# A four-layer graph network on one core: layer 0 of the first batches by the adjacency itself, zero products while it loads, another order of loads

## The chip, the core and the metric

The kernel runs on one core of a Trainium2 chip. The core has a matrix engine (TensorE, PE in the profile, with its weight loads as PEld), a vector engine (DVE), a scalar engine (ACT), GpSimd (POOL), a sync engine (SP) that here only issues transfers, and 16 DMA engines behind the queues of SP and ACT. All data is float32, but for the masks (bfloat16). The metric is the device time of one run in microseconds, lower is better. Three runs of the kernel before took 1646.48, 1648.0 and 1648.28 us.

## The reference

`x` is 32 batches of 512 nodes with 128 features, `adj` one 512 x 512 matrix, mostly zeros, positive where there is an edge, the diagonal included. Four layers follow one another, each as `x = x + layer(relu(layernorm(x)))`. Layer 0 is the one that the change touches:

```python
A_hat = adj + eye(n)
d = sum(A_hat, axis=-1) ** (-0.5)
A_norm = d[:, None] * A_hat * d[None, :]
out = einsum('nm,bmc->bnc', A_norm, x)
out = einsum('bnc,oc->bno', out, W) + b
```

Layer 1 is a gated graph unit of five steps; each step multiplies `adj` with the state `h` of a batch and puts the result and `h` through gates: `z = sigmoid(..)`, `r = sigmoid(..)`, `hv = tanh(.. + (r*h) @ u5.T)`, `h = (1-z)*h + z*hv`. Layers 2 and 3 are graph attention: `e = leaky_relu(e_src + e_dst)`, masked by `adj`, softmax over the neighbours, and the weighted sum of `h = x @ W`; layer 2 has an elu behind it.

## The kernel before

**Tiles.** The 512 nodes of a batch lie as four chunks of 128 partitions, so a batch is a tile of 128 x (4 x 128). `adj` is loaded as four chunks of 128 rows (L250, on the queues of SP and ACT in turn), and PE turns each chunk, block by block, into `adjT` (L285; ACT copies the result out of PSUM, L287). Beside it DVE sums the rows to `deg` (L288, L290), and GpSimd raises it to the power -0.5: `dinv` (L291).

**The normalized matrix.** Before layer 0 can start, `anT`, the turned A_norm, is built: PE turns `dinv` into a row spread over all partitions (L300), and for each of four chunks DVE multiplies `adjT` by `dinv` of the partition and by that row (L308) and adds dinv squared on the diagonal block (L311).

**Layer 0** (`gcn`) works on pairs of batches. Normalization takes the statistics on DVE (L406, L410, L411), the reciprocal root on GpSimd (L413), an offset on DVE (L420) and the scaled relu on ACT (L423). The first two pairs (batches 0 to 3) use `product`: four matmuls of 128x128 by 128x512 each (L551), one PSUM copy on ACT (L553), four small matmuls by the turned W (L572) and one addition into x on DVE (L574). All later pairs use `products`, which makes both batches of a pair at once by seven products of half size in place of eight (L516); it needs sums and differences of the halves of its two inputs, the tile `S` (L504, four DVE operations), and sums of quarters of the matrix, `made` (L325). Layer 1 (`ggnn`, `step`) uses `products` with `adjT` in each of its five steps, then the gate matmuls (L603, L604, L610, L617 and, for the candidate, L618), tanh on ACT (L606, L612, L620) and the update on DVE (L608, L622, L623, L625). At the end of layer 1 the result is added to x (L633 for the last batches).

**Attention** (`gat`) makes scores from a row of values and the masks (e, L713), multiplies (L733, for the last four batches L722), and adds the result into x (L738, L750, L752 in layer 2; L744 in layer 3). The masks are made once (L340, L342) and go through DRAM (L345, L348) to `maskT`.

**Order.** The program has no fixed loop order. `Plan` collects operations with an engine, a cost, a due time, and the values that they read and write; a value takes a buffer from a small pool when its first operation starts (two tiles `y`, eight PSUM banks, thirteen `x`). `run` walks through this list as an event queue: on each engine the ready operation with the earliest due time goes next. It tries 16 settings of two parameters, keeps the one that ends first by its own costs, and emits the instructions in that order. Each engine then executes its own list strictly in order, and an instruction that waits holds up all behind it. So a change of a cost or a due time anywhere can move operations everywhere, and the order of transfers on SP is such a list as well. Transposes of weights (`transposed`, L364, with the copies L368 and L370) and small constants have due times from -1000 to -9 and fill the start; x of batches 0 to 7 has due times from -995 on.

Of the kernel before, what the change touches and what calls it, by code (L numbers as in the profile page):

```python
# [12 lines left out]
AF = mybir.ActivationFunctionType  # L13
ALU = mybir.AluOpType

P = 128
# [5 lines left out]
NEAR = 4  # L22
EASE = 0
FAR0, FAR1 = 2, 4
LANES = 6


# [140 lines left out]
def gnn_stack(ctx: ExitStack, tc: tile.TileContext, a: dict, out: bass.AP):  # L168
# [13 lines left out]
    def flat(t):  # L182
        return t.rearrange("p c k -> p (c k)")
# [54 lines left out]

    ident = fixed([P, P], "ident")
    mhalf = fixed(SMALL, "mhalf")  # L240
    warm = fixed([P, 1], "warm")
    op("POOL", 0.8, -1000, lambda: make_identity(nc, ident.t), w=[ident])
    op("POOL", 0.1, -999, lambda: nc.gpsimd.memset(mhalf.t, -0.5), w=[mhalf])
    op("DVE", 0.1, -1000, lambda: nc.vector.memset(warm.t, 0.0), w=[warm])
    op("ACT", 1.4, -1000, lambda: nc.scalar.activation(warm.t, warm.t, AF.Tanh), w=[warm])

    adj_sb = Val("e", C)
    for c in range(C):
        e, q = (("SP", nc.sync), ("ACT", nc.scalar))[c % 2]
        op(e, 0.45, -1001, lambda c=c, q=q: q.dma_start(adj_sb.t[:, c, :], adj[c * P:(c + 1) * P, :]),  # L250
           w=[adj_sb[c]], delay=3.6)
    xs = []
    for b in range(B):
        v = Val("x", C)
        op("SP", 0.95, max(-995 + b, STEPS * b - 20) if b >= 8 else -995 + b, lambda v=v, b=b: nc.sync.dma_start(v.t, x[b].rearrange("(c p) d -> p c d", p=P)),
           w=[v], delay=3)
        xs.append(v)
    w0 = load("w0", [P, D], a["L0_gnn_W"], -993.5)
    b0 = load("b0", [P, D], bass.AP(tensor=a["L0_gnn_b"].tensor, offset=a["L0_gnn_b"].offset,
                                    ap=[[0, P], [1, D]]), -993.4)  # L260

# [6 lines left out]
    w_aug, a_pair = {}, {}  # L268
    for l, w in ((2, "L2_gnn_W"), (3, "L3_gnn_w")):
        w_aug[l] = fixed([P, D + 3], f"w_aug{l}", 2)  # L270
        op("SP", 0.45, -990.5, lambda l=l, w=w: nc.sync.dma_start(w_aug[l].t[:, :D], a[w]), w=[w_aug[l][0]], delay=2.4)
        a_pair[l] = fixed([P, 2], f"a_pair{l}", 2)
        for i, k in enumerate(("src", "dst")):
            op("SP", 0.45, -990.4, lambda l=l, i=i, k=k: nc.sync.dma_start(
                a_pair[l].t[:, i:i + 1], column(a[f"L{l}_gnn_a_{k}"])), w=[a_pair[l][i]], delay=2.4)
# [4 lines left out]
    for c in range(C):  # L280
        p = Val("bank")

        def turn_adj(c=c, p=p):
            for m in range(C):
                nc.tensor.transpose(p.t[:, m, :], adj_sb.t[:, c, m * P:(m + 1) * P], ident.t)  # L285
        op("PE", C * TURN, -800, turn_adj, r=[adj_sb[c], ident], w=[p])
        op("ACT", A, -800, lambda c=c, p=p: nc.scalar.copy(adjT.t[:, :, c * P:(c + 1) * P], p.t), r=[p], w=[adjT[c]])  # L287
        op("DVE", 0.66, -801, lambda c=c: nc.vector.reduce_sum(deg.t[:, c:c + 1], adj_sb.t[:, c, :], axis=mybir.AxisListType.X),  # L288
           r=[adj_sb[c]], w=[deg[c]])
    op("DVE", 0.1, -799, lambda: nc.vector.tensor_scalar_add(deg.t, deg.t, 1.0), w=[deg])  # L290
    op("POOL", 1.0, -1000, lambda: nc.gpsimd.tensor_tensor(dinv.t, deg.t, mhalf.t, ALU.pow), r=[deg, mhalf], w=[dinv])  # L291


    anT = fixed([P, C, N], "anT", C)
    drow = Val("bank")
    dinv2 = fixed(SMALL, "dinv2")

    def turn_dinv():
        for c in range(C):
            nc.tensor.transpose(drow.t[:, c, :], dinv.t[:, c:c + 1].to_broadcast([P, P]), ident.t)  # L300
    op("PE", C * TURN, -798, turn_dinv, r=[dinv, ident], w=[drow])
    op("DVE", 0.1, -798, lambda: nc.vector.tensor_mul(dinv2.t, dinv.t, dinv.t), r=[dinv], w=[dinv2])

    def block(t, m):
        return t[:, m, m * P:(m + 1) * P]

    for m in range(C):
        op("DVE", 0.7, -797, lambda m=m: nc.vector.scalar_tensor_tensor(  # L308
            anT.t[:, m, :], adjT.t[:, m, :], dinv.t[:, m:m + 1], flat(drow.t), op0=ALU.mult, op1=ALU.mult),
           r=[adjT, dinv, drow], w=[anT[m]])  # L310
        op("DVE", 0.26, -797, lambda m=m: nc.vector.scalar_tensor_tensor(  # L311
            block(anT.t, m), ident.t, dinv2.t[:, m:m + 1], block(anT.t, m), op0=ALU.mult, op1=ALU.add),
           r=[ident, dinv2], w=[anT[m]])

    def right_factors(mT, due):

# [9 lines left out]
                f[k][0](), quarter(*u), quarter(0, 1) if v is None else f[v][0]()),  # L326
               r=[mT, *([f[v][1]] if v else [])], w=[f[k][1]])
        return f
    of_adj, of_an = right_factors(adjT, -3), right_factors(anT, 5)


    maskT = {l: fixed([P, Q, N], f"maskT{l}", C, dtype=BF16) for l in (2, 3)}
    for l in (2, 3):
        far = Val(None, C)
        far.t = tiles(1, [Q, W, C, N], f"far_mask{l}", dram, BF16)[0]
        for c in range(C):
            part = Val("mask", 1)

            def edges(l=l, c=c, part=part):
                nc.vector.tensor_scalar(part.t, adjT.t[:, c, :], 0.0, None, op0=ALU.is_gt)  # L340
                if l == 2:
                    nc.vector.scalar_tensor_tensor(part.t[:, c * P:(c + 1) * P], block(adjT.t, c), -1.0, ident.t,  # L342
                                                   op0=ALU.mult, op1=ALU.is_lt)
            op("DVE", 0.35 if l == 3 else 0.6, 4 + l, edges, r=[adjT, ident], w=[part])
            op("SP", 0.4, 4 + l, lambda c=c, far=far, part=part: nc.sync.dma_start(  # L345
                far.t[:, :, c, :].rearrange("q i n -> (q i) n"), part.t), r=[part], w=[far[c]], delay=2.2)
        for c in range(C):
            op("SP", 0.4, 4 + l, lambda l=l, c=c, far=far: nc.sync.dma_start(  # L348
                maskT[l].t[c * W:(c + 1) * W], far.t[:, :, c, :].rearrange("q i n -> i q n")),
               r=[far], w=[maskT[l][c]], delay=2.2)  # L350

# [27 lines left out]
    w0T = transposed(-750, (one(w0), 1))  # L379
    gates = transposed(-700, (halves("w4"), 1), (one(raw["u3"]), 1), (halves("w3") + halves("w4", minus), 1), (halves("w5"), 1))  # L380
    u5T = transposed(-690, (one(raw["u5"]), 0.5))
    gats = transposed(-10, (one(w_aug[2]), 1), (one(w_aug[3]), 1))
    gate_b = {}
    for k, u, half in (("w4", "u3", True), ("w3", "u3", True), ("w5", "u5", False)):
        gate_b[k] = fixed([P, 1], "gate_b" + k)
# [5 lines left out]

    for i, l in enumerate((2, 3)):
        p = Val("bank")
        op("PE", 0.3, -9, lambda i=i, l=l, p=p: nc.tensor.matmul(p.t[:, 0, :2], gats.t[:, i, :], a_pair[l].t, start=True, stop=True),
           r=[gats, a_pair[l]], w=[p])

        def columns(l=l, p=p):
            for j, (s, f) in enumerate(((1, SLOPE), (1, 1.0 - SLOPE), (0, SLOPE - 1.0))):
                nc.vector.tensor_scalar_mul(w_aug[l].t[:, D + j:D + j + 1], p.t[:, 0, s:s + 1], f)
        op("DVE", 0.3, -9, columns, r=[p], w=[w_aug[l][1]])  # L400


    def norm_stats(b, due):
# [9 lines left out]
        op("POOL", 1.0, due, lambda: nc.gpsimd.tensor_tensor(rstd.t, ve.t, mhalf.t, ALU.pow), r=[ve, mhalf], w=[rstd])  # L413
        return mv, rstd

    def norm_relu(b, y, due):

        xb, off = xs[b], Val("off")
        mv, rstd = norm_stats(b, due)
        op("DVE", 0.1, due, lambda: nc.vector.scalar_tensor_tensor(off.t, mv.t[:, :, 0], -1.0, rstd.t, op0=ALU.mult, op1=ALU.mult),  # L420
           r=[mv, rstd], w=[off])
        for c in range(C):
            op("ACT", 0.385, due, lambda c=c: nc.scalar.activation(  # L423
                chunk(y, c), xb.t[:, c, :], AF.Relu, bias=off.t[:, c:c + 1], scale=rstd.t[:, c:c + 1]),
               r=[xb[c], off, rstd], w=[y[c * len(y.writers) // C]])
# [118 lines left out]
        copy(m1[1], r, lambda: high(m1))  # L544
        return m1, m2

    def product(h, mT, due):

        p, m = Val("bank"), Val("m")
        for c in range(C):  # L550
            op("PE", MM, due, lambda c=c: nc.tensor.matmul(flat(p.t), chunk(h, c), mT.t[:, c, :], start=(c == 0), stop=(c == C - 1)),  # L551
               r=[h[c], mT[c]], w=[p, m])
        op("ACT", A, due, lambda: nc.scalar.copy(flat(m.t), flat(p.t)), r=[p], w=[m])  # L553
        return m


    def gcn(pair, due):
        first, ys = pair[0] < 4, []
        for i, b in enumerate(pair):
            y = Val("y", C) if first else Val("pair", 2)  # L560
            norm_relu(b, y, 2 * b - 798 if pair[0] == 0 else due + i)
            op("DVE", V, due + i + 1, lambda b=b: nc.vector.tensor_add(
                xs[b].t, xs[b].t, b0.t[:, None, :].to_broadcast([P, C, D])), r=[b0], w=[xs[b]])
            ys.append(y)

        ms = [product(y, anT, due + i + 1) for i, y in enumerate(ys)] if first else products(*ys, of_an, due + 1)
        for i, (b, m) in enumerate(zip(pair, ms)):
            p = Val("bank")

            def out_mm(m=m, p=p):  # L570
                for c in range(C):
                    nc.tensor.matmul(p.t[:, c, :], m.t[:, c, :], w0T.t[:, 0, :], start=True, stop=True)  # L572
            op("PE", C * MM1, due + i + 1.5, out_mm, r=[m, w0T], w=[p])
            op("DVE", V, due + i + 1.5, lambda b=b, p=p: nc.vector.tensor_add(flat(xs[b].t), flat(xs[b].t), flat(p.t)),  # L574
               r=[p], w=[xs[b]])


    def ggnn(pair, due):
# [177 lines left out]


    for b in range(0, B, 2):
        gcn((b, b + 1), STEPS * b - 10)
        ggnn((b, b + 1), STEPS * b)  # L760
        for i in range(2):
            gat(b + i, 2, STEPS * (b + i) + LANES * (STEPS - 1) + 3)
# [33 lines left out]
```

The softmax here doesn't subtract the row's maximum and nothing guards it: scores larger than these inputs give would overflow.

## Time and profile before

| | |
|---|---|
| time of three runs | 1646.48 to 1648.28 us, median 1648.0 |
| span of the profiled run | 1645.1 us |
| PE busy | 1620.7 us, 99% |
| DVE busy | 1373.5 us, 83% |
| ACT busy | 722.0 us, 44% |
| first PE instruction | 4.64 us |
| last PE instruction ends | 1640.1 us |

A line of the time line gives start, duration (from the start of the first to the end of the last of a run of like instructions), engine, line, operation, output and input with shapes, and how many; a bracket gives the idle time of the engine before it and what ended that. PE's instructions overlap, so the cost of one is read from start to start and not from its duration. A line of waits gives the sum, the number and the longest, in us. A line of the table by stretch gives from and to, its length, busy time and instructions of PE, PEld, DVE, ACT and POOL, then the granted clock of PE, the DMA share and GB/s.

### The profile page before, as it was taken

The page shows a single profiled execution, that of the slowest core. Times are in us where ns is not written, and L with a number is a line of the kernel's source. Part 1 is how long each engine was busy: PE and PEld are TensorE (multiplying, and loading weights), DVE is VectorE, ACT ScalarE, POOL GpSimd, SP SyncE. Part 2 cuts the span into 40 slices and gives each one's busy share as a digit, 9 for nine tenths or more (in the row PEclk, how much of TensorE's full clock was granted, in tenths as well). Part 3 has the DMA queues.
Part 4 walks back from the last instruction along what each step waited for, and adds up shares of the span by engine and source line. Part 5 has one row for each costly group of instructions (what it writes and reads, how often), then busy time and mean ns, then how long its engine had stood idle before and what let it go on. Part 6 is the DMA issues. An engine that isn't in the chain of part 4 may idle for free.

```text
span 1645.1 us, 23871 instructions
## 1 busy us (share of the span) xinstructions
PE 1620.7 (99%) x7306; PEld 1159.8 (71%) x7306; DVE 1373.5 (83%) x3881; ACT 722.0 (44%) x1629; POOL 144.6 (9%) x136
## 2 busy tenths in 40 slices
PE   8999999999999999999999999999999999999997
PEld 5666666777767677776776677767777777666776
DVE  8977587888878898888888898888888887788887
ACT  4643353534345443544534444353443534443433
POOL 2200010110101110000100100110000000000000
PEclk9999999999999999999999999999999999999999
DMA  5433253444535344453434535334363422434100
GB/s 148 109 73 72 53 127 93 104 106 105 124 78 136 90 106 106 102 134 86 113 95 100 129 90 142 87 94 113 91 143 76 114 68 72 122 91 103 46 20 26
DMA packets 381312, 159.81 MB, mean 97 GB/s; under 512 B 206976, under 2 KB 362752, under 8 KB 381184
## 3 DMA queue, kind: packets, MB, share of 16 engines
q1 hardware_dynamic: 380896, 157.77, 39.4%
q8 instruction: 58, 0.95, 0.2%
q14 instruction: 70, 0.57, 0.1%
q10 hardware_dynamic: 288, 0.52, 0.1%
HBM read 87.30 MB, written 70.89 MB: 96 GB/s over the span
## 4 chain that ended last, share of the span: by engine, by line
PE 94%; DVE 4%; DMA 1%; issue 0%; ACT 0%; SPq 0%; DVEq 0%
PE bank L516 34%; PE bank L733 12%; PE bank L603 8%; PE bank L604 8%; PE bank L617 8%; PE bank L610 8%; PE bank L618 8%; PE bank L678 3%; PE bank L572 1%; PE bank L722 1%; DVE e L713 1%; DVE st L406 1%; PE bank L705 0%; PE bank L448 0%; DVE y L432 0%
## 5 line engine op out<-in xcount | busy, mean ns | idle before, releaser
L413 POOL TENSOR_TENSOR rstd<-ve,mhalf 128x4 f32<-128x4 f32 x128 | 142.8, 1117 | 1473.4 <-DVE ve L411 1166.1
L516 PE MATMUL bank<-made,S 128*128 128x256 f32 x1128 | 270.3, 380 | 1.6 <-DVE S L504 0.7
L516 PEld LDWEIGHTS bank<-made,S 128*128 128x128 f32 x1128 | 217.3, 196 | 42.2 <-issue 18.6
L733 PEld LDWEIGHTS bank<-h_gat,e 128*128 128x128 f32 x1792 | 208.2, 192 | 17.4 <-issue 14.8
L521 ACT COPY half<-bank 128x256 f32<-128x256 f32 x282 | 104.6, 371 | 246.6 <-PE bank L516 239.1
L733 PE MATMUL bank<-h_gat,e 128*128 128x129 f32 x1792 | 209.0, 275 | 0.0
L606 ACT ACTIVATE r<-bank,gate_bw 128x512 f32<-128x512 f32 x160 | 109.6, 685 | 205.2 <-PE bank L604 186.5
L713 DVE SCALAR_TENSOR_TENSOR e<-row,h_gat,maskT 128x512 f32<-128x512 f32 x256 | 182.7, 742 | 0.0
L608 DVE SCALAR_TENSOR_TENSOR rh<-r,hT 128x512 f32<-128x512 f32 x160 | 109.9, 687 | 76.5 <-ACT r L606 75.6
L622 DVE TENSOR_TENSOR hv<-hv,hT 128x512 f32<-128x512 f32 x160 | 109.6, 685 | 75.9 <-ACT hv L620 75.3
L620 ACT ACTIVATE hv<-bank,gate_bw 128x512 f32<-128x512 f32 x160 | 109.5, 684 | 126.7 <-PE bank L618 125.6
L610 PE MATMUL bank<-m,wT 128*128 128x512 f32 x320 | 163.8, 593 | 0.0
L617 PE MATMUL bank<-m,wT 128*128 128x512 f32 x320 | 163.7, 593 | 0.0
L603 PE MATMUL bank<-m,wT 128*128 128x512 f32 x320 | 163.5, 592 | 0.0
L618 PE MATMUL bank<-rh,wT 128*128 128x512 f32 x320 | 163.4, 592 | 0.0
L604 PE MATMUL bank<-hT,wT 128*128 128x512 f32 x320 | 163.4, 592 | 0.0
L516 PE MATMUL bank<-adjT,h 128*128 128x256 f32 x640 | 161.6, 380 | 0.6 <-ACT h L423 0.3
L529 DVE TENSOR_TENSOR m<-half,bank 128x256 f32<-128x256 f32 x282 | 116.1, 413 | 33.2 <-ACT half L521 15.7
L516 PEld LDWEIGHTS bank<-adjT,h 128*128 128x128 f32 x640 | 121.2, 196 | 26.7 <-issue 11.3
L612 ACT ACTIVATE z<-bank,gate_bw 128x512 f32<-128x512 f32 x160 | 109.3, 683 | 53.8 <-PE bank L610 51.5
L406 DVE BATCH_NORM_STATS2 st<-x 128x6 f32<-128x128 f32 x512 | 121.5, 279 | 1.5 <-DMA x<-in_x_dram 0.6
L423 ACT ACTIVATE y<-x,off,rstd 128x128 f32<-128x128 f32 x240 | 104.5, 485 | 26.9 <-DVE off L420 25.0
(117 smaller groups left out, 2182.5 us busy)
## 6 DMA issues: line engine op xcount, KB each, us to landing
far<-sq SPq DMA_DIRECT2D x936, 64.0 KB
h<-far SPq DMA_DIRECT2D x248, 128.0 KB
gT<-far SPq DMA_DIRECT2D x56, 256.0 KB
row<-line SPq DMA_DIRECT2D x56, 256.0 KB
x<-in_x_dram SPq DMA_DIRECT2D x32, 256.0 KB
out_dram<-x SPq DMA_DIRECT2D x32, 256.0 KB
h<-far SPq DMA_DIRECT2D x28, 256.0 KB
hT<-far SPq DMA_DIRECT2D x104, 64.0 KB
```

The costliest lines, as they stand in the source:

```text
L406: op("DVE", 0.21, due, lambda c=c: nc.vector.bn_stats(st.t[:, c, :], xb.t[:, c, :]), r=[xb[c]], w=[st[c]])
L413: op("POOL", 1.0, due, lambda: nc.gpsimd.tensor_tensor(rstd.t, ve.t, mhalf.t, ALU.pow), r=[ve, mhalf], w=[rstd])
L516: nc.tensor.matmul(low(r), u[:, l, :], factors[k][0]()[:, l, :], start=fresh and l == 0, stop=l == 1, skip_group_check=not fresh)
L529: op("DVE", HV, due - 5, lambda: nc.vector.tensor_add(out(), u.t, low(t)), r=[u, t], w=[o])
L603: nc.tensor.matmul(flat(gate.t), gates.t[:, 0, :], flat(m.t), start=True, stop=False)
L604: nc.tensor.matmul(flat(gate.t), gates.t[:, 1, :], flat(hT.t), start=False, stop=True)
L608: op("DVE", V, due - 5, lambda: nc.vector.scalar_tensor_tensor(flat(rh.t), flat(r.t), 1.0, flat(hT.t), op0=ALU.add, op1=ALU.mult), r=[r, h ...
L610: op("PE", MM, due + 0.3, lambda: nc.tensor.matmul(flat(gate.t), gates.t[:, 2, :], flat(m.t), start=False, stop=True, skip_group_check=Tru ...
L617: nc.tensor.matmul(flat(cand.t), gates.t[:, 3, :], flat(m.t), start=True, stop=False)
L618: nc.tensor.matmul(flat(cand.t), u5T.t[:, 0, :], flat(rh.t), start=False, stop=True)
L713: op("DVE", 0.68, due + 3, lambda j=j: nc.vector.scalar_tensor_tensor(e.t[:, j, :], row.t, h.t[:, j, D + 1:D + 2], maskT[l].t[:, j, :], op ...
L733: nc.tensor.matmul(pt()[:, c, :D + 1], e.t[:, j, i * P:(i + 1) * P], h.t[:, j, :D + 1], start=(j == 0), stop=(j == C - 1))
```

## The change

The aim is to let PE start useful work earlier in the run.

- **Layer 0 of batches 0 to 3 without `anT`.** A_norm h is written as D (A + I) (D h), with D the diagonal of `dinv`. The rows of h are scaled by `dinv` (for batch 0 in two DVE steps, for batches 1 to 3 by putting `dinv` into the scale of the relu), the product takes `adjT` itself, with four small tiles `diag` (the diagonal blocks plus the identity) in place of its diagonal blocks, and the sum into x multiplies by `dinv` chunk by chunk. A product is then ten matmuls in place of four. `anT` is still built, for the later pairs, but with a later due time.
- **Zero products.** Eight 128x128 products of zeros go to PE while `adj` loads.
- **Loads.** x of batch 0 is the first transfer on SP, and the chunks of `adj` change their queues; w0 comes a little earlier. The cost given to the planner for an x transfer is 0.5 in place of 0.95.
- **Degrees.** Two of the four row sums go to ACT, as a copy with an accumulated output.
- **Later.** Masks are due at 14 + l in place of 4 + l, the columns of the attention weights at 10 in place of -9, and the second pair's layer 0 six steps earlier.

```diff
+RUN_UP = 8
...
+    run_up = Val("bank")
+
+    def turn_nothing():
+        for _ in range(RUN_UP):
+            nc.tensor.matmul(run_up.t[:, 0, :], warm.t[:, 0, :], warm.t[:, 0, :], start=True, stop=True)
+    op("PE", 0.43 * RUN_UP, -1002, turn_nothing, r=[warm], w=[run_up])
...
-        op("SP", 0.95, max(-995 + b, STEPS * b - 20) if b >= 8 else -995 + b, lambda v=v, b=b: nc.sync.dma_start(v.t, x[b].rearrange("(c p) d -> p c d", p=P)),
-           w=[v], delay=3)
+        op("SP", 0.5, -1002 if b == 0 else max(-995 + b, STEPS * b - 20) if b >= 8 else -995 + b,
+           lambda v=v, b=b: nc.sync.dma_start(v.t, x[b].rearrange("(c p) d -> p c d", p=P)), w=[v], delay=3)
...
+        e, q = (("ACT", nc.scalar), ("SP", nc.sync))[c % 2]
...
-    w0 = load("w0", [P, D], a["L0_gnn_W"], -993.5)
+    w0 = load("w0", [P, D], a["L0_gnn_W"], -994.5)
...
+        if c < 2:
+            junk = Val("r")
+            op("ACT", 0.7, -801, lambda c=c, junk=junk: nc.scalar.activation(
+                flat(junk.t), adj_sb.t[:, c, :], AF.Copy, accum_out=deg.t[:, c:c + 1]), r=[adj_sb[c]], w=[junk, deg[c]])
...
+    diag = Val("v", C)
     for m in range(C):
...
+        op("DVE", 0.16, -799.5, lambda m=m: nc.vector.tensor_add(diag.t[:, m, :], block(adjT.t, m), ident.t),
+           r=[adjT[m], ident], w=[diag[m]])
...
-            op("DVE", 0.35 if l == 3 else 0.6, 4 + l, edges, r=[adjT, ident], w=[part])
+            op("DVE", 0.35 if l == 3 else 0.6, 14 + l, edges, r=[adjT, ident], w=[part])
...
+        if times:
+            op("DVE", 0.1, due, lambda: nc.vector.tensor_mul(rstd.t, rstd.t, times.t), r=[times], w=[rstd])
...
+            def times(c=c):
+                for lo, hi in ((0, c), (c, c + 1), (c + 1, C)):
+                    if lo < hi:
+                        right = diag.t[:, c, :] if lo == c else adjT.t[:, c, lo * P:hi * P]
+                        nc.tensor.matmul(flat(p.t)[:, lo * P:hi * P], h.t[:, c, :], right, start=c == lo == 0, stop=c == C - 1,
+                                         skip_group_check=True)
...
+        op("PE", C * TURN, -2, turn_dinv, r=[dinv, ident, begun], w=[drow])
...
+            if b == 0:
+                norm(b, y, -802)
+                for c in range(C):
+                    op("DVE", 0.16, -800, lambda c=c, y=y: nc.vector.tensor_scalar(
+                        y.t[:, c, :], y.t[:, c, :], 0.0, dinv.t[:, c:c + 1], op0=ALU.max, op1=ALU.mult), r=[dinv], w=[y[c]])
+            else:
+                norm_relu(b, y, -798 if b == 1 else due + i, dinv if first else None)
...
-        ms = [product(y, anT, due + i + 1) for i, y in enumerate(ys)] if first else products(*ys, of_an, due + 1)
+        ms = [product(y, due + i) for i, y in enumerate(ys)] if first else products(*ys, factors["an"], due + 1)
+        if b == 1:
+            factors["an"] = normalized(ms[0])
...
+            if first:
+                for c in range(C):
+                    op("DVE", 0.26, due + i + 1.5, lambda b=b, c=c, p=p: nc.vector.scalar_tensor_tensor(
+                        xs[b].t[:, c, :], p.t[:, c, :], dinv.t[:, c:c + 1], xs[b].t[:, c, :], op0=ALU.mult, op1=ALU.add),
+                       r=[p, dinv], w=[xs[b][c]])
...
-        gcn((b, b + 1), STEPS * b - 10)
+        gcn((b, b + 1), STEPS * b - (16 if b == 2 else 10))
```

## The prediction

> **What bounds the kernel now.** I read first the busy shares of the page, then the time line of the first 20 us, the table of busy time by stretch, the waits of TensorE (PE), and last the time line of the end.
>
> ```profile
> PE 1620.7 (99%) x7306; PEld 1159.8 (71%) x7306; DVE 1373.5 (83%) x3881; ACT 722.0 (44%) x1629; POOL 144.6 (9%) x136
> ```
>
> PE is the bound over the span, so time can come only from places where PE stands still, runs slowly, or has more or less to do. A row of PE is a record; a float32 matmul makes two, a transpose one. In the middle, two records of 128x512 start every 0.86 us (L610 at 42.85, L617 at 43.70), a record of 128x128 costs 0.111 (four from 11.02 to 11.46) and one of 128x256 0.216. At these prices the whole order of PE is about 1609 us of work; 36 us of the span are something else. Where the first of them lie:
>
> ```profile
> 4.53 1.28 DVE L288 TENSOR_REDUCE deg<-e 128x1 f32<-128x512 f32 x2 [3.66 <-DMA e<-in_adj_dram]
> 4.64 3.65 PE L285 MATMUL bank<-ident,e 128*128 128x128 f32 x16 [4.64 <-DMA e<-in_adj_dram]
> ...
> 7.73 1.02 POOL L291 TENSOR_TENSOR dinv<-deg,mhalf 128x4 f32<-128x4 f32 x1 [6.38 <-DVE deg L290]
> ...
> 8.19 2.54 PE L364 MATMUL bank<-ident,w 128*128 128x128 f32 x10
> ...
> 11.02 0.61 PE L364 MATMUL bank<-ident,w 128*128 128x128 f32 x4
> ...
> 11.46 0.60 PE L300 MATMUL bank<-ident,dinv 128*128 128x128 f32 x4
> ...
> 12.18 0.75 DVE L308 SCALAR_TENSOR_TENSOR anT<-adjT,dinv,bank 128x512 f32<-128x512 f32 x1 [2.51 <-PE bank L300]
> ...
> 14.06 3.80 PE L551 MATMUL bank<-anT,y 128*128 128x512 f32 x8 [1.55 <-DVE anT L311]
> ```
>
> Two things are to be seen. The first product (L551) starts at 14.06, behind a chain of transposes, dinv, dinv turned to a row (L300, which itself stands behind slow weight transposes) and four pairs of L308 and L311. And 16 transposes took 3.65 us, 0.228 each, twice the 0.111 of the same shape at 11.02: PE ran at half rate until about 10.6, though the next rows give the granted clock (the 1.00 ahead of the DMA share) as full.
>
> ```profile
> 0.00:4.64 4.64, 0.00 (x1) 0.03 (x1) 0.17 (x2) 1.69 (x3) 0.75 (x7) 1.00 0.59 177
> 4.64:10.57 5.93, 5.93 (x26) 5.60 (x27) 4.77 (x20) 2.60 (x5) 2.03 (x2) 1.00 1.05 306
> ```
>
> The 26 records there cost 0.117 too much each, 3.0 us in all. Up to 60.14 us PE has done 45.9 us of work at the prices above: 14.2 us are lost in the start. From 14 us on the vector engine (DVE) is the second bound: it is busy over nine tenths up to 40 us. The rest of the large waits lies at the end:
>
> ```profile
> PE bank L722 <- DVE e L713: 5.0, 4, 3.1
> ```
>
> After the last candidate matmul (L618, ends at 1593.7) come 51.4 us with 324 records, only 36.5 us of work; there DVE leads.
>
> **What the Trainium skill says.** "TensorE: Matmul & The Clock Gate", Part 1, has the array start at half clock and go to full after about 3.4 us of sustained work, in a window that runs freely, so that the moment varies. The trace agrees on the factor (0.228 against 0.111) and shows a longer time, 5.9 us from the first record. "DMA: Bandwidth & Descriptors", Issuing engines are not separate DMA queues, says that transfers of the sync and scalar queues share the same engines; the 306 GB/s of 4.64 to 10.57 with a DMA share of 1.05 fits: another order moves transfers, it does not make them shorter. "VectorE: DVE Perf Modes", TRN2 errata, says that each operation carries a fixed extra latency, so small pieces cost more: four L744 on 128x128 took 1.09, one L574 on 128x512 0.69 (0.60 from start to start).
>
> **The change, part by part.** Times below are 128x128 DVE pieces at 0.19 (L432, two in 0.4), 128x512 at 0.60.
>
> *Loads.* x of batch 0 (262 KB) now goes ahead of two chunks of adj on the sync queue. By the rates of the first six us (29, 162, 369, 404, 349 GB/s) adj alone (1049 KB) was moved by 5.3 and its last chunks were seen at 6.0 to 6.7, a lag of about 1. Adj and x together (1311 KB) are moved at 6.0, so the last chunk is there at about 7.0: 0.7 later. In the new order of PE the transpose of w0 stands second, before three of the four chunks; w0 lies behind adj in its queue, so PE waits for it to about 7.2.
>
> *Zero products.* Eight, 16 records at 0.228: 3.65 us, from the memset (done at about 1) to 4.7, where PE stood idle: no cost. They may start the clock. Bounds: it is full from 4.7 (all 3.0 us saved), or, because PE waits again for w0, only at 10 to 13 (1.8 us of the next figure lost). I take the fast case at about two in three.
>
> *The path to the first product.* Three chunks of transposes from 7.4 at 0.45 each: 8.8. Five groups of weight transposes, 22 records, 2.45 us; the last weight (2228 KB moved, at the old rates 9.1 plus 1) is there at 10, so they end at about 11.0 to 11.3. Beside it: the last copy of adjT on ACT (0.58) ends at 9.7, deg at 8, dinv (1.02) at 9.4, the diagonal blocks 0.19 each, and four pieces of y from 10.2. So the product starts at about 11.3 against 14.06, and runs without the two gaps of before (3.43 us for eight records against 3.64): 3.0 us won; at half rate 1.2.
>
> *Splitting the product.* Ten matmuls for four, with the same columns: 48 records more in all (7306 to 7354 without the zeros). A 128x128 pair costs 0.224 against 0.2145 for a quarter of a 512 one: 0.06 a product, 0.25 us in all.
>
> *DVE.* Removed from the start: two reduces (1.24, to ACT). Moved later: L308 and L311 (3.7 us), and masks. Added: four diagonal pieces and eight for y of batch 0 (2.3), and four out-adds in four pieces (1.08 for 0.60: 1.9). Summed in the new order, DVE has about 44.0 us of work before the S of the second pair (first GRU step, batches 2 and 3), which the PE order wants after 41.8 us of its own. DVE enters with about 5 us idle behind it and loses 1 to 1.5 more on rstd and on PE, so this S comes at about 50.5; PE, 7.0 us behind its ideal when the first product ends (14.7 against 7.7), arrives at 48.8. A wait of about 2, and the same again at the S of the pair after it (about 1.9; before: 0.65 and 0.46). PE is then 10.5 to 11.5 behind, before 14.3. So the start keeps 2.8 to 3.8; with a third for the half-rate case I take 2.7.
>
> *Masks later, gats and columns later, deg on ACT.* Off the path: the masks are read only in the attention layers some 30 us on, and PE has full work then.
>
> *The end.* The planner orders everything anew. After the last candidate matmul 340 records (38.3 us) are left in the new order, 324 (36.5) before: PE arrives there 1.6 us earlier, besides the start, and 1.8 us of work goes into a stretch with 10 us of idle. From the last layer-1 add (L633, 4.5 us after it) DVE has 30.2 us to the first e of the last batch, before 28.8; but before, DVE also stood behind PE (5.6 us), which I find less of in the new order (2 to 4). I count the stretch at 51.4 as before, from 49.5 to 54.
>
> *Sum.* 2.7 + 1.6 - 0 = 4.3; the split is in both terms. 1648.0 - 4.3 = 1643.7.
>
> **Rivals.** (A) The forecast, 1643.7. (B) The head start is given back: PE is not short of its own work but of what DVE makes, so the earlier product only means longer waits at S. For it: DVE over nine tenths busy up to 40 us; against: 3.7 us of anT leave the head of the queue. At half rate (1.2 won) and with 1 us more of waits nothing is left of the start, and the end gives 1 to 2: about 1647. (C) Slower: the end or the middle comes out worse. The longest wait for e is 3.1 us; two such more, and the half-rate start with waits of 4 at S: 1648 - 1.2 + 1.5 + 6.2 - 1.6 = 1653. For it: the whole order is new, about four tenths of PE's rows stand elsewhere; against: between 60 and 1590 us PE shows only 3.0 us of waits, with an order made in the same way. (D) More than forecast: full clock from 4.7, no new waits at S (3.8 more), end at 49.5: about 1638.
>
> **How the numbers follow.** A 0.55, B 0.25, C 0.12, D 0.08. The bound of 0.2% is 3.3 us: faster means below 1644.7. A lies only 1 us beyond it and D well, some of A falls short and a little of B reaches it: faster 0.6, same 0.28, slower 0.12. The range: A is open by 2 us at the clock, 2 at S and 2 to 3 at the end, so 1639 to 1649 leaves out most of C and half of D, about two in ten.
>
> **What would show it.** First product at 11 to 11.5 (12.5 to 13 if the clock is late, with transposes at 0.228 after 5 us); PE waiting for w0's load; waits for S near 48 and 55 us of about 2 each; L308 after 30 us; about 51 us after the last candidate. Wrong: a w0 or x later than 8 us, a wait above 4 at S, or waits of PE in the middle well over 3 us.

## The result, and the profile after

The changed kernel takes 1653.5 us (median of six runs, 1652.0 to 1655.7) against 1648.1 us before: ratio 1.0035, 95% interval 1.0022 to 1.0048. It is 5.4 us slower, where 4.3 us less were forecast. The case that came true is rival C, at its time. Of its reasons, the one that held is "the whole order is new"; the waits of its sum (two more for e, 4 us at S) did not come.

First the busy shares of the page of the changed kernel, then its time line of PE up to the first product:

```profile
PE 1626.7 (99%) x7370; PEld 1168.0 (71%) x7370; DVE 1372.9 (83%) x3905; ACT 721.4 (44%) x1629; POOL 145.3 (9%) x136
```

```profile
1.05 3.78 PE L252 MATMUL bank<-hv 128*128 128x128 f32 x16 [1.05 <-DVE hv L245]
4.62 1.06 PE L293 MATMUL bank<-ident,e 128*128 128x128 f32 x4
7.12 0.49 PE L364 MATMUL bank<-ident,w 128*128 128x128 f32 x2 [1.43 <-DMA w<-in_L_gnn_W_dram]
7.45 1.47 PE L293 MATMUL bank<-ident,e 128*128 128x128 f32 x12
...
10.99 0.39 PE L557 MATMUL bank<-v,y 128*128 128x128 f32 x2
```

PE has 64 records more: 16 of zeros (L252) and 48 of the divided products, as counted in advance. The start went as forecast: PE waits for w0 until 7.12 (forecast 7.2), twelve transposes take 1.31 us from start to next start, 0.11 each, so the clock is full, and the first product starts at 10.99 (forecast 11.3, before 14.06). The clock was not full before that wait: the zero products and the first four transposes stand 0.21 apart, the rate that the kernel before has up to 10.57. It rose while PE waited for w0. Behind the first product, forecast and trace part. At 67 us the time line, DVE and PE together, shows this:

```profile
67.29 0.76 DVE L340 TENSOR_SCALAR mask<-adjT 128x512 bf16<-128x512 f32 x2 [2.44 <-DMA far_mask<-mask]
...
71.04 0.42 DVE L506 TENSOR_TENSOR S<-h,h 128x256 f32<-128x256 f32 x1
...
71.52 1.14 PE L518 MATMUL bank<-made,S 128*128 128x256 f32 x4 [2.06 <-DVE S L506]
```

The vector engine (DVE) stands 2.44 us in front of a mask part, because one of the only two mask buffers is still being read by the transfer to DRAM (L345), which lies in the queue of SP between the transfers of layer 1. All that stands behind the mask on DVE is late, S among it, and PE waits 2.06 us for S. Before, the same wait of DVE was shorter and earlier, and PE did not wait in the nine microseconds behind it:

```profile
44.46 0.43 DVE L340 TENSOR_SCALAR mask<-adjT 128x512 bf16<-128x512 f32 x1 [0.88 <-DMA far_mask<-mask]
```

Between 80 and 200 us three more waits for the copy `half` appear than before, each of 0.46 us; by the starts of the records each costs PE 0.62:

```profile
94.70 2.00 PE L518 MATMUL bank<-made,S 128*128 128x256 f32 x8 [0.46 <-ACT half L523]
104.14 1.14 PE L518 MATMUL bank<-made,S 128*128 128x256 f32 x4 [0.46 <-ACT half L523]
105.74 1.14 PE L518 MATMUL bank<-adjT,S 128*128 128x256 f32 x4 [0.46 <-ACT half L523]
```

Then nothing of size until 1500 us. The first line is all that PE waited for in the kernel before from 1490 to 1560 us; the rest is the changed kernel:

```profile
PE bank L516 <- ACT half L521: 0.9, 2, 0.5
...
1502.74 1.95 PE L518 MATMUL bank<-adjT,h 128*128 128x256 f32 x8
...
1503.66 0.69 DVE L666 TENSOR_TENSOR hv<-hv,hT 128x512 f32<-128x512 f32 x1 [0.68 <-ACT hv L664]
...
1504.39 0.69 DVE L667 SCALAR_TENSOR_TENSOR hv<-z,hv 128x512 f32<-128x512 f32 x1
...
1505.00 0.41 DVE L531 TENSOR_TENSOR m<-half,bank 128x256 f32<-128x256 f32 x1
1505.33 0.68 DVE L669 SCALAR_TENSOR_TENSOR hT<-hv,hT 128x512 f32<-128x512 f32 x1
...
1505.94 0.41 DVE L506 TENSOR_TENSOR S<-h,h 128x256 f32<-128x256 f32 x1
...
1506.40 1.14 PE L518 MATMUL bank<-made,S 128*128 128x256 f32 x4 [1.71 <-DVE S L506]
```

```profile
1506.40:1510.23 3.83, 3.09 (x8) 1.79 (x8) 1.70 (x5) 0.37 (x1) 0.00 (x0) 0.70 0.76 247
1510.23:1512.36 2.13, 1.67 (x4) 1.09 (x4) 0.02 (x1) 0.37 (x1) 0.00 (x0) 0.74 0.58 134
```

In the new order S stands on DVE behind the update of the other batch (L666, L667, L669), and PE has nothing but this product to do. The table by stretch (its third column from the end is the granted clock) shows more: the mean clock behind the wait is 0.70 to 0.74 for six microseconds. By the starts of the records, PE is at full rate at first. From 1507.8 on, behind a further wait of 0.28 us, it is at half rate (0.43 for 256 columns in place of 0.216) up to about 1511.3, and then at full rate again.

"Lost" below is the time of day less the work that PE has done by then (in microseconds; zero products are not work). The prices are those of the prediction: 0.111 for a record of up to 131 columns, 0.216 for 256, 0.43 for 512, and 0.323 for the 384 columns that only the changed kernel has.

| lost up to | 50 | 60 | 80 | 200 | 1500 | 1550 | 1600 | end |
|---|---|---|---|---|---|---|---|---|
| before | 12.6 | 14.3 | 14.8 | 15.9 | 19.0 | 20.5 | 22.6 | 32.5 |
| after | 9.2 | 12.0 | 14.4 | 17.5 | 20.5 | 26.2 | 28.0 | 37.4 |

So 3.4 us are won by 50 us and 2.3 of them are left at 60; by 200 us they are gone and 1.6 more; between 1500 and 1550 the changed kernel loses 4.2 more than the one before; the last stretch costs about what it did (waits for e fell, those for v and y came):

```profile
PE bank L766 <- DVE e L757: 1.5, 2, 1.1
PE bank L450 <- DVE v L782: 1.2, 1, 1.2
PE bank L450 <- DVE y L434: 0.8, 2, 0.4
```

Three causes could be behind it: (M) the masks put off into layer 1's transfers, (N) the new order as such, which the planner makes of any changed number, (B) a start in which DVE takes back whatever head start PE gets.

### The profile page after: what moved, and what is told of

It reads as the page before. It is cut to its first block, busy times and chain, and to the rows that moved or that the text cites. A ratio compares the mean times of both kernels' runs of the same rounds, so it can differ in the third digit from the quotient of the medians.

```text
span 1650.2 us, 24013 instructions
## 1 busy us (share of the span) xinstructions
PE 1626.7 (99%) x7370; PEld 1168.0 (71%) x7370; DVE 1372.9 (83%) x3905; ACT 721.4 (44%) x1629; POOL 145.3 (9%) x136
## 4 chain that ended last, share of the span: by engine, by line
PE 92%; DVE 5%; DMA 1%; ACT 1%; issue 0%; SPq 0%; POOL 0%; DVEq 0%; POOLq 0%; ACTq 0%
PE bank L518 33%; PE bank L777 12%; PE bank L661 8%; PE bank L647 8%; PE bank L662 8%; PE bank L648 8%; PE bank L654 8%; PE bank L722 3%; PE bank L610 2%; PE bank L766 1%; DVE st L406 1%; DVE S L506 0%; PE bank L450 0%; DVE e L757 0%; PE bank L749 0%
## 5 line engine op out<-in xcount | busy, mean ns | idle before, releaser
L518 PE MATMUL bank<-made,S 128*128 128x256 f32 x1128 | 274.5, 382 | 8.8 <-DVE S L506 4.5
L666 DVE TENSOR_TENSOR hv<-hv,hT 128x512 f32<-128x512 f32 x160 | 109.4, 684 | 70.0 <-ACT hv L664 69.3
L662 PE MATMUL bank<-rh,wT 128*128 128x512 f32 x320 | 163.4, 592 | 0.0
L662 PEld LDWEIGHTS bank<-rh,wT 128*128 128x128 f32 x320 | 60.8, 190 | 76.5 <-issue 67.0
```

The costliest lines, as they stand in the source:

```text
L518: nc.tensor.matmul(low(r), u[:, l, :], factors[k][0]()[:, l, :], start=fresh and l == 0, stop=l == 1, skip_group_check=not fresh)
L662: nc.tensor.matmul(flat(cand.t), u5T.t[:, 0, :], flat(rh.t), start=False, stop=True)
```

## The experiments

All times are medians, with the ratio to the kernel before, run beside it on the same chip, and its 95% interval. The ratio is formed from all executions and need not be the quotient of two medians. Line numbers shift by the lines added. Of each edit the lines that matter are shown; "..." stands for the rest.

### Single parts undone or done alone

**e1: masks in places of their own.** The order stays; the eight parts lie in a buffer that is empty until the attention layers.

```diff
+    idle = plan.buffers["e"][-1]
...
+        for i, v in enumerate(parts):
+            v.t = idle[:, i // 2, i % 2 * 256:(i % 2 + 1) * 256].bitcast(BF16)
```

> The changed kernel with its order of instructions kept; only the eight mask parts get a place of their own (in a buffer that stands empty until the attention layers), so that none waits for an earlier part's transfer to land. Theory M (the masks, put off into the transfers of layer 1, cost the start its gain): the vector engine no longer stands 2.4 us before the third mask part near 67 us, the wait of PE for S near 71.5 us (2.06 us in the changed kernel) falls under 0.5, and the time goes from 1653.5 to about 1651.5. Rival (the vector engine simply has too much to do there, and S is late whoever waits): the wait of PE stays at 1.5 or more and the time stays within 0.5 us of 1653.5.

Measured: 1649.4, 1.0012 [1.0005, 1.0018], 4.1 us less than the changed kernel. With the same order, instruction can be set beside instruction: at 66 us PE is 0.96 later than in the changed kernel's trace, at 71.5 it is 1.27 earlier. So the mask's buffer costs 2.2 us there, and the wait of PE for S at that place is gone. The lead stays at 1.4 to 1506 us; there, behind the same wait of 1.72 us, the clock stays full in this run, and the lead is 2.8 from 1515 on. M is right on the wait; that the time fell by more than 2.2 can be that clock, and lies within the intervals.

The start of this trace has something to show as well:

```profile
4.63 1.06 PE L294 MATMUL bank<-ident,e 128*128 128x128 f32 x4
7.04 0.80 PE L372 MATMUL bank<-ident,w 128*128 128x128 f32 x2 [1.35 <-DMA w<-in_L_gnn_W_dram]
7.63 2.59 PE L294 MATMUL bank<-ident,e 128*128 128x128 f32 x12
```

The same twelve transposes at 0.20 each, and the first product at 12.29. Ahead of the wait the two traces are alike: zero products and four transposes 0.21 apart. So the clock did not fall back here; it had not risen yet, and rose at 9.8 us. Of the five traces with just this start (the changed kernel, e1, e3, e5, e7), two had the full clock behind the wait, with the first product at 10.96 and 10.99, and three the half, with 12.2 to 12.5.

**e2: without the zero products.**

```diff
-        for _ in range(RUN_UP):
+        for _ in range(0):
```

> The changed kernel without the eight zero products, same order. Both theories: the transposes of adj run at half rate (0.22 us each) and the first product starts 1.5 to 3 us later than at 10.99. Theory P (a head start of PE is kept to the end): 1655 to 1656.5. Theory B (the head start is given back to the vector engine by 75 us whatever its size): 1653.5, within 0.7.

Measured: 1654.2, 1.0043 [1.0031, 1.0056]. First product at 12.58, against 11.0 where the clock rose in time with the zero products and 12.2 to 12.5 where it did not. The median is nearer to the expectation of B, but five executions from 1652.9 to 1655.9 do not tell it from P.

**e3: from 300 us on the old order.** Each operation is ranked by a table: up to 300 us by its place in the changed kernel's plan, then by that in the plan of before, and PE and DVE keep strictly to the table.

```diff
...
-            o.soon = min(o.due, last - o.tail * hurry)
+            o.soon = min(o.due, last - o.tail * hurry) if pins is None else pins[o.id]
```

> The changed kernel up to 300 us in its own order; from there on the instructions of TensorE and of the vector engine stand in the order of the kernel before. Theory R (4.2 us of the loss are the newly planned order between 1500 and 1552 us, with a wait for S of 1.7 us and a slow clock behind it): that stretch loses no more than before (1.5 us), and the time is about 1649.3. Rival (the loss comes from the start, and the late stretch only passes it on or loses the like in any order): 1652.5 to 1653.5.

Measured: 1651.1, 1.0026 [1.0016, 1.0035]: 2.4 less, not 4.2. The wait at 1506 is gone, and the stretch 1500 to 1550 loses 1.0 (1.5 before, 5.7 in the changed kernel). But the old order has its 4.7 us of waits for e behind it at the end, where the new one has 1.5. About half of what the late stretch gives is returned there.

**e4: the zero products alone, on the kernel before.**

```diff
...
+        nc.vector.memset(zeros, 0.0)
+        for _ in range(8):
+            nc.tensor.matmul(spare[:, 0, :], zeros, zeros, start=True, stop=True)
```

> The kernel before with nothing added but the eight zero products and the clearing of what they read, in front of everything else, same order. Both theories: the 26 records up to 10.6 us run at full rate, and the first product comes earlier than 14.06, by at most 3.0 us, less where it stands behind loads and the vector engine. Theory P (a head start of PE is kept): 1645 to 1646.5. Theory B (the vector engine takes it back): 1647.5 to 1648.2.

Measured: 1647.7, 1.0001 [0.9993, 1.0009]. The product comes at 13.14 in place of 14.06, and instruction by instruction PE is 1.33 us ahead from 55 us up to 1600 us: DVE does not take it back. It goes in the last 45 us, with nearly the same waits, behind two falls of the clock. The first two rows are the kernel before, the others this run:

```profile
1600.00:1605.00 5.00, 3.83 (x25) 3.01 (x26) 4.96 (x20) 1.83 (x5) 1.03 (x1) 1.00 0.00 0
1625.00:1630.00 5.00, 4.67 (x41) 4.36 (x41) 2.46 (x7) 2.56 (x9) 0.00 (x0) 1.00 0.00 0
...
1600.00:1605.00 5.00, 4.54 (x24) 4.27 (x24) 5.00 (x14) 2.06 (x5) 0.38 (x1) 0.66 0.00 0
1620.00:1625.00 5.00, 1.90 (x10) 1.77 (x9) 4.93 (x25) 0.74 (x2) 2.52 (x2) 0.71 0.00 0
1625.00:1630.00 5.00, 5.00 (x30) 5.00 (x30) 2.22 (x6) 1.19 (x2) 0.00 (x0) 0.61 0.00 0
```

So B names the wrong taker. P is right on the trace up to 1600 us and wrong on the time. Only this execution was traced, one of the long ones (1648.8); of the thirteen none took less than 1646.5, and what takes the lead back in the short ones is not shown.

### Two at a time, and the order

**e5: e1 and e3 together** (both edits as above).

> The two edits of the first set together: each mask part in a place of its own, and from 300 us on the order of the kernel before. Theory M and R (two separate losses): the savings add up, 1653.5 - 4.1 - 2.4 = about 1647.0. Rival (both runs saved the same thing, slow clock or waits that come back at the end): 1649 to 1651.

Measured: 1650.0, 1.0013 [1.0005, 1.0020], no better than e1 alone. PE is 1.8 ahead of e3 from 75 to 1605 us, and 0.3 behind it at the end, with a clock of 0.50 between 1625 and 1630. The rival: in this trace, what was saved comes back at the end.

**e6: masks late, alone, in the order of before.** The edit is that of e3 with another table, here written in short.

```python
TABLE = {k: places_before[k] for k in places_before}
TABLE["masks"] = places_after["masks"]
```

> The kernel before, its order kept; only the making of the masks (vector engine) and their transfers stand as late as in the changed kernel (the last parts near 60 to 70 us in place of 31 to 45). Theory M (masks between the transfers of layer 1 cost the wait for the buffer and make S late): a wait of the vector engine for a mask's transfer of 1.5 us or more, a wait of PE for S of 1 to 2.5 us behind it, and 1649 to 1650.5. Rival (masks are off the path, as the prediction had it): no wait of PE over 0.7 us behind a mask, 1647.5 to 1648.3.

Measured: 1650.4, 1.0018 [1.0010, 1.0027]: 2.5 us, as M expects, but by another way. DVE does not wait for a mask's transfer. The masks stand in front of what PE needs (time line, DVE and PE):

```profile
66.83 0.42 DVE L372 TENSOR_SCALAR mask<-adjT 128x512 bf16<-128x512 f32 x1
...
67.51 0.42 DVE L372 TENSOR_SCALAR mask<-adjT 128x512 bf16<-128x512 f32 x1
67.84 0.41 DVE L562 TENSOR_TENSOR m<-half,bank 128x256 f32<-128x256 f32 x1
...
68.31 2.00 PE L549 MATMUL bank<-made,S 128*128 128x256 f32 x8 [0.93 <-DVE m L562]
```

PE waits 0.33, 0.43 and 0.93 between 56 and 69 us and falls from 0.3 ahead of before (at 55) to 1.7 behind (at 70); it is still 1.7 behind at 1600, and 3.5 at the end of this trace. So late masks cost by their place on DVE too, without any wait for their buffer.

**e7: S ahead at 1503 us.** e1, with one more move in the list of DVE: the four L506 of this pair go ahead of L666 of the other batch, or as near to it as their inputs allow.

```diff
+        for i in [8118, 8119, 8120, 8121]:
+            o = ops[i]
+            self.order.remove(o)
+            at = max([self.order.index(ops[7745])] + [self.order.index(p) + 1 for p in self.ops if o in p.then])
+            self.order.insert(at, o)
```

> The changed kernel with the masks in places of their own (1649.4), and one more move: near 1503 us the four operations that make S stand ahead of the state update (L666, L667, L669) and of the adding of m (L531) on the vector engine, where they stood behind. Theory R1 (the wait of 1.7 us near 1506 us is the place of S in the queue of the vector engine): it falls under 0.7 and the time to about 1647.5, lower by up to 1.5 more where the slow clock behind the wait goes too. Rival (the inputs of S, the states that come back by transfer, are late themselves): the vector engine now waits for them, the wait of PE stays over 1.2, 1649 to 1650.5.

Measured: 1649.2, 1.0011 [1.0005, 1.0018], as e1. The wait for S is gone; PE's time line has another in its place, for the operation that now stands behind:

```profile
1504.14 2.00 PE L532 MATMUL bank<-made,S 128*128 128x256 f32 x8 [1.56 <-DVE m L545]
```

Neither theory: S was late by its place, but in this stretch PE is fed by one pair only, and what it waits for is the next link of DVE's chain. This single move did not mend it.

**e8: one number of the planner, on the kernel before.**

```diff
-        op("SP", 0.95, max(-995 + b, STEPS * b - 20) if b >= 8 else -995 + b, ...
+        op("SP", 0.5, max(-995 + b, STEPS * b - 20) if b >= 8 else -995 + b, ...
```

> The kernel before with one number of the planner changed, the cost of a transfer of x from 0.95 to 0.5, as in the changed kernel; no instruction is added or removed, the planner merely orders anew (about three in ten of PE's rows stand elsewhere). Theory N (a new order alone moves the time by some us, whatever caused it): off 1648 by 1.5 us or more, to either side. Rival (the planner's orders are equally good, and the loss belongs to the other edits): 1647.3 to 1648.7.

Measured: 1653.8, 1.0044 [1.0031, 1.0056]. The same instructions, the whole loss. PE's waits of this run from 1490 to 1560 us are like those of the changed kernel:

```profile
PE bank L516 <- DVE S L504: 2.0, 2, 1.7
PE bank L516 <- ACT half L521: 1.8, 4, 0.5
```

They are not all of it. "Lost" is 0.4 below that of the kernel before at 200 us, 3.4 above at 1500 (waits for `half` at 279, 281, 567 and 605 us above all), 6.2 at 1550 and 7.0 at the end. In this trace the clock stays full behind the wait at 1508 us.

**e9: the changed kernel with that number put back.**

```diff
-        op("SP", 0.5, -1002 if b == 0 else ...
+        op("SP", 0.95, -1002 if b == 0 else ...
```

> The changed kernel with one number put back: the planner's cost of a transfer of x at 0.95, as before; the same instructions, ordered anew. Theory N (the new order that the number caused is most of the loss): the wait for S of 1.7 us near 1506 us is gone, and the time is 1653.5 - 5.9 = about 1648, by the run that changed this number alone; since this is again another order, 1646 to 1650. Rival (masks and the divided start cost the most, in any order): 1652 to 1655.

Measured: 1648.1, 1.0003 [0.9995, 1.0012]: the loss of 5.4 us is gone. The start is better as well: "lost" at 200 us is 11.1, in the changed kernel 17.5, on the same instructions. From 1490 to 1560 us one line of waits is left for PE:

```profile
PE bank L518 <- ACT half L523: 0.9, 2, 0.5
```

Against the changed kernel, this order wins 6.4 us by 200 us and 4.2 between 1500 and 1550; it gives 3.5 back between 200 and 1500 and 3.7 behind 1550. That is the 3.4 us by which the two traced executions differ (1648.6 and 1652.0).

**e10: e9 with the masks in places of their own.**

> The same with each mask part in a place of its own. Theory N and M together: 1653.5 - 5.9 - 4.1 = 1643.5 at best, 2 to 4 us below the run with the old number alone, if a wait for a mask's transfer stands in that one; what the edits to layer 0 were to bring would then be there. Rival (a head start does not reach the end): 1647 or more.

Measured: 1647.3, 1.0000 [0.9992, 1.0008]. The masks give 0.8 here (in e9 DVE waits only 0.7 us for a mask's buffer). The rival: the head start does not reach the end. But it is there: "lost" at 200 us is 10.6 against 15.9 before, so it is 5.3 us and larger than forecast. It goes later, by waits for the copy `half` that the old order has not; the time line of PE at the largest:

```profile
274.36 1.14 PE L526 MATMUL bank<-made,S 128*128 128x256 f32 x4 [0.81 <-ACT half L531]
275.96 1.14 PE L526 MATMUL bank<-adjT,S 128*128 128x256 f32 x4 [0.46 <-ACT half L531]
```

Two more stand at 561 and 599 us. With 0.16 us for starting up again, the four cost 2.8 us. What is left, 2.0 us at 1500, goes at the end, where the clock is at 0.66 from 1600 to 1605 and from 1625 to 1630 us.

**e11: more zero products in the wait for w0**, on e1.

```diff
...
+    def turn_more():
+        for _ in range(8):
+            nc.tensor.matmul(plan.buffers["bank"][-1][:, 0, :], warm.t[:, 0, :], warm.t[:, 0, :], start=True, stop=True)
```

> The changed kernel with the masks in places of their own (1649.4), and eight more zero products between the first transposes of adj and the transpose of w0, where PE otherwise stands 1.4 us. Theory C (that wait lets the clock fall back in some executions, and in the one looked at): all transposes at 0.11 us, the first product at 11.0 in place of 12.3. If the 1.3 us are kept: 1648.1. Rival (the lead is lost in the last 50 us, as with the zero products before): the first product early all the same, 1649 to 1649.8.

Measured: 1649.3, 1.0012 [1.0005, 1.0019]. First product at 11.00, and full rate behind the wait, as C says. But the run doesn't show that the added products did it. Its time line up to the wait:

```profile
1.05 3.47 PE L255 MATMUL bank<-hv 128*128 128x128 f32 x16 [1.05 <-DVE hv L248]
4.36 0.60 PE L300 MATMUL bank<-ident,e 128*128 128x128 f32 x4
4.80 1.95 PE L258 MATMUL bank<-hv 128*128 128x128 f32 x16
```

The first transposes take 0.60 in place of 1.06: here the clock was full from 4.1 us, ahead of the added products (L258). The rival on the time: PE is 1.1 us ahead of e1 at 200 and 0.6 from 400 to 1506 us, and there, in this run, the clock falls to 0.50 behind the wait for S, and 2.7 us are lost.

### Where a head start stays

**e12: the start of e10, the order of before.** With the old number and own masks, the first 80 us keep their plan, and from there on the ranks are those of before; about one in twenty of PE's operations stands elsewhere than before. The table, written in short:

```python
TABLE[k] = [y if y >= 80 else x for x, y in zip(places_e10[k], places_before[k])]
```

> The changed kernel with the old cost of a transfer of x and the masks in places of their own, its order kept for the first 80 us, and from there on ranked as in the kernel before (about one in twenty of PE's rows stands elsewhere than before). Theory G (the head start of 4.4 us at 200 us in the run with the old cost is lost to the waits of 0.6 to 1.0 us for copies near 275, 561 and 599 us that the new order has and the old has not, and then to the clock): PE enters the last 50 us 3 to 4 us ahead of the kernel before, and the time is 1644 to 1645.5. Rival (the end gives back whatever lead there is): 1646.5 to 1648.

Measured: 1643.0, 0.9977 [0.9968, 0.9987]. PE is 5.1 to 5.5 us ahead of before from 400 to 1616 us, but for single places where rows differ. At the end 3.4 are left, by the clock in this run:

```profile
1615.00:1620.00 5.00, 1.93 (x10) 1.68 (x9) 4.93 (x25) 0.87 (x3) 2.52 (x2) 0.66 0.00 0
1620.00:1625.00 5.00, 5.00 (x32) 5.00 (x32) 2.32 (x6) 1.19 (x2) 0.00 (x0) 0.66 0.02 3
```

**e13: waits of the end filled, on the kernel before.** The five numbers of `FILL` stand for an L448, an L678, an L698 and two L722.

```diff
+FILL = {8235: 2, 7890: 3, 7896: 2, 7902: 12, 8284: 4}
...
+    plan.nothing = lambda n, t: [nc.tensor.matmul(t[:, 0, :], ident.t, ident.t, start=True, stop=True) for _ in range(n)]
```

> The kernel before, same order, with 23 small products that nothing reads, ahead of five instructions of PE that wait for other engines between 1600 and 1633 us (2, 3, 2, 12 and 4 of them, each shorter in sum than the wait there). Theory C (the granted clock falls behind those waits, near 1602 and 1622 us, in most executions, and that is a part of the time): clock 1.00 throughout the last 50 us, and 1645 to 1646.5. Rival (the vector engine sets the end, the slow clock lies beside it): 1647.5 to 1648.5; over 1648.5 if the products delay what waits.

Measured: 1646.0, 0.9990 [0.9982, 0.9999]: 1.7 us. The clock is 1.00 in every stretch from 1595 to 1640 us. The executions show where the gain comes from. Those of the kernel before, run beside it, lie between 1646.1 and 1649.2 us, and the longer ones have the lower mean clock (0.998 to 0.999 up to 1647.2, 0.997 from 1648.6 on). Those of e13 lie between 1645.5 and 1646.6, with 0.998 to 1.000. So the long executions are gone, and the shortest is little shorter.

**e14: both.**

> Both together. Theories G and C: 1641.5 to 1643.5, faster than both kernels. If only one holds: 1644 to 1646. If neither: 1647 to 1648.

Measured: 1641.9, 0.9968 [0.9956, 0.9981]. Its rows to those of e12:

```profile
1615.00:1620.00 5.00, 4.61 (x42) 4.42 (x40) 4.93 (x25) 0.85 (x3) 2.52 (x2) 1.00 0.01 3
1620.00:1625.00 5.00, 4.67 (x41) 4.36 (x40) 2.30 (x6) 2.73 (x10) 0.00 (x0) 1.00 0.00 0
```

It is the fastest of all, 5.8 us under the kernel before and 11.6 under the changed one. On the same instructions it gains 1.7 on e12 behind the wait for e; the medians differ by 1.1, with intervals that overlap.

## Why the prediction was wrong

**The step that failed** is the one taken against rival C: "between 60 and 1590 us PE shows only 3.0 us of waits, with an order made in the same way". From it the sum had nothing for the middle. But an order made in the same way is not one as good. One changed cost (0.95 to 0.5 for x), which the prediction does not cost at all, gives an order that is 5.9 us worse with no instruction changed (e8), and putting it back takes off 5.4 (e9). In the changed kernel PE waits 8.5 us between 60 and 1590 us, by the same view that showed 3.0 before.

In the terms of the sum: of the 2.7 us for the start, 2.3 were there at 60 us. Then come losses that the sum had at nothing, each beyond what the kernel before loses in the same stretch: 1.9 us from 60 to 80 (the mask), 2.0 from 80 to 200 (three waits for copies) and 4.2 from 1500 to 1550 (a wait of 1.7 for S, one of 0.28 for S, two of 0.46 for copies, and the slow clock). The "+1.6" came: 340 records are left behind the last candidate, as counted. But with the losses the last L662 ends at 1598.0, 4.3 us later than before.

**Masks later**, costed at nothing with "PE has full work then", is the second step that failed. The reader of a mask was checked, not what the mask holds up: two buffers, freed by transfers that now queue among those of layer 1, and DVE in order. By e6, it is 2.5 us in the order of before; in the changed kernel it is 2.2 us at one wait (e1). The work named as hiding it is work that DVE feeds.

**What held.** The path to the first product to 0.3 us, the zero products' place, the wait for w0, the count of records, the last stretch (51.4 counted, 52.2 measured from the last candidate to the end of the span). The 0.3 us are in part luck: the clock rose in time in two of five traces with this start. The rate of the slow transposes was read a little too high: 0.228 is the duration of sixteen divided by sixteen, with the tail of the last; from start to start they stand 0.213 apart. The two waits at S were mis-sized: 1.08 for m, 0.46 and 0.49 between 52 and 57 us in place of about 2 and 1.9; what came instead was the 2.06 at 71.5 behind the mask. What the edits to the start can bring was put too low: with the old number and the masks in places of their own it is 5.3 us at 200 us (e10), and 4.7 us of it reach the end in e12.

**Not additive, and partly open.** The number (5.9), the masks (2.5) and the rest (-4.7) sum to 3.7 where 5.4 were measured; each order has its own waits, and the intervals are 3 to 4 us wide. Why this number yields this order was not traced through the planner, and no other number was tried. The number also moves the transfers and the operations of ACT; which engine's list carries the loss was not told apart. That the clock has a share in the end is shown by e13 and e14, only for orders that end like the one of before.

**The clock.** The Trainium skill, "TensorE: Matmul & The Clock Gate", Part 1, says that the window in which activity is watched runs freely; the runs agree: behind the same zero products the full rate came at 4.0 us in one run (e9) and at 10.3 in another (e5), and behind the same wait at 1506 us the clock stayed full in e1 and fell to half in the changed kernel. The same page, Why this matters for your kernels, puts the limit at gaps of about 3 us; here a gap of 1.7 us and one of 0.28 behind it were enough in three of the five traces that have them (the changed kernel, e2 and e11; not in e1 and e8), so the measurement decides. The prediction left the clock at "two in three" for the start, and did not think of it behind other waits, where it doubles the price of the next few microseconds of PE's work.

## What to carry to other kernels

Where a planner orders the program, the edit and the new order are two changes: run the planner's changed numbers alone on the old instructions, and the edit in the old order, before judging either. For an operation that is put off, ask not only when its result is needed but whose queue it stands in and what frees its buffer. A head start of PE counts in full only if the waits at the end do not also cost it the clock; here, small products that nothing reads, put into those waits, kept it (e13, e14).

## What was not expected of the hardware

The granted clock falls behind short waits and then stays at half for some microseconds: about 3.5 us in the changed kernel (1507.8 to 1511.3), 6.4 in e11 at the same place, 5.1 in e12. At the end, first in e12, then in e14:

```profile
1618.34 3.81 PE L807 MATMUL bank<-h_gat,e 128*128 128x129 f32 x16 [3.08 <-DVE e L798]
...
1615.08 2.84 PE L291 MATMUL bank<-ident 128*128 128x128 f32 x24
1618.31 2.05 PE L825 MATMUL bank<-h_gat,e 128*128 128x129 f32 x16 [0.39 <-DVE e L816]
```

Behind the wait of 3.1 us for e, the sixteen records of 128x129 took 0.22 each in e12 (3.6 us to the next start at 1621.94), and 0.12 in e14 (to 1620.20), where 24 records of unread products had filled the wait. All the fillings together, some 5 us of PE time, made the kernel faster.

At the start, no fall of the clock behind a wait is shown, for it had not risen yet. Behind the same eight zero products from 1.05 us on, the full rate came anywhere between 4.0 us (e9) and 10.3 us (e5).
